# Cross attention: GpSimd in written order too, the rows' scale three steps ahead, a set's quotient ahead of its step's sums

## The chip, the cores and the metric

The kernel runs on one core of a Trainium2 chip. The metric is device time in microseconds of one execution, the median of several. Five engines work side by side, each through its own queue in order: TensorE (PE; its weight loads are listed as PEld), VectorE (DVE), ScalarE (ACT), GpSimd (POOL) and SyncE (SP), which here only issues transfers.

## What is computed

One decoder layer on x of 4 x 512 x 512 (2048 rows), in three blocks, each added to the residual:

```python
x = x + attn(layernorm(x))            # causal, window of 128, 16 heads, sink, folded output weights
x = x + xattn(layernorm(x), ctx)      # 16 query heads in 4 groups, 1024 keys, 4 batches
x = x + ffn(layernorm(x))             # ternary weights, 8-bit rows, silu gate, Hadamard turn
```

The middle block is the one that the change touches:

```python
Q, K, V = query @ Wq, key @ Wk, value @ Wv        # 16 heads of 32 over 4 groups of keys and values
scores = einsum(Q / sqrt(32), K) + slope * (k - q)  # masked keys to the least number
out = einsum(softmax(scores), V) @ Wo
```

Ahead of it and ahead of the feed-forward block each row is normalized, (x - mean) / sqrt(var + 1e-5).

## The kernel before, in words

The work of the cross attention is cut into 16 sets: set m is batch m // 4 and head hh = m % 4 of all four groups, with its 512 queries. A set has 8 tiles of 128 keys. The main loop (line 1295) takes one tile a step: step = 8 m + kt, written here as m.kt, so that step 9 is 1.1.

In a step TensorE computes scores transposed (keys on the partitions) into two score buffers (`st`, lines 1100 and 1111), ScalarE takes their exponentials `p` (line 1118, two instructions of 128 x 1024), and TensorE weighs the values with those of the step before (line 1136). GpSimd adds the exponentials of a set's tiles 1 to 7 into two sums (line 1125, two additions a step; in the last set VectorE does it). For a set further on TensorE also makes untransposed scores (line 1038, four a step), of which VectorE takes row maxima (line 1042). They are turned, copied by ScalarE and sent as two more rows of the queries (`shift`, lines 1077 to 1093), so that the exponentials can't overflow.

In step m.1 the sums of set m - 1 are added over the keys by TensorE (`divide`), copied by ScalarE, and spread by transfers; in m.2 VectorE takes reciprocals, which return by transfers; in m.4 GpSimd multiplies the set's output by them (`quotients`, line 1183). Later `output` (line 1190) multiplies by Wo and VectorE adds to the residual.

Work for later stages is laid between these steps by `plan`: turning the next batch's context, its keys and values, the queries of later sets, and two kinds of normalized rows. `rows_of(b)` (line 270) is a generator that prepares the next batch's four row tiles; each `next` runs it to its next `yield`. Its parts are: the statistics on VectorE (lines 87 and 88), `norm_of` (line 100), which has GpSimd add epsilon (`veps`, line 106) and take the power -0.5 (`rstd`, the scale of the rows, line 80); then `norm_shift` (line 110), in which ScalarE computes -mean x scale (`shift`, lines 113 and 116), for which it needs GpSimd's result; then the rows themselves (`norm_rows`, line 120), each turned by TensorE a step later. `ffn_rows` (line 331) does the same for pairs of row tiles of the feed-forward block, with three steps between `norm_of` and `norm_shift`, and then quantizes the rows; six pairs start at steps 87, 93, 102, 108, 114 and 120, which are 10.7, 11.5, 12.6, 13.4, 14.2 and 15.0.

What sets the order on an engine is `tc.manual_schedule(engines=...)`, line 1274. An engine named there issues in the order in which the program is written. For the others a planner, with its own estimates of each instruction's time, places instructions by when it believes them to be ready, and may move them ahead of what is written before them. In the kernel before only TensorE is named in the cross attention. Whatever the order, each engine's queue is worked off from the front, and an instruction that waits for another engine's result holds all behind it.

Of the kernel before, what the change touches and what calls it, by code (L numbers as in the profile page):

```python
# [50 lines left out]
def decoder_layer(  # L51
# [48 lines left out]
    def norm_of(t0, n):  # L100

        mv = row_stats(t0, n)
        veps, rstd, shift = (
            small.tile([P, QT], F32, name=name, bufs=1) for name in ("veps2", "rstd2", "shift")
        )
        nc.gpsimd.tensor_tensor(veps[:, :n], mv[:, :n, 1], least[:, 0, :n], ALU.add)
        power_neg_half(rstd[:, :n], veps[:, :n])
        return mv, rstd, shift, n

    def norm_shift(mv, rstd, shift, n):  # L110

        for i in range(n):
            nc.scalar.activation(
                shift[:, i:i + 1], mv[:, i, 0:1], AF.Copy, scale=rstd[:, i:i + 1]
            )
        nc.scalar.activation(shift[:, :n], shift[:, :n], AF.Copy, scale=-1.0)
        return rstd, shift

    def norm_rows(dst, t, i, rstd, shift):
        nc.scalar.activation(  # L120
            dst, xres[:, t, :], AF.Identity, bias=shift[:, i:i + 1], scale=rstd[:, i:i + 1]
        )
# [66 lines left out]
    def transpose4(src, dst, copy):  # L189
        ps = some_bank([P, DC, P], "tr_ps")  # L190
        for c in range(DC):
            nc.tensor.transpose(ps[:, c, :], src[:, ts(c, P)], ident)
        copy(dst, ps)
# [73 lines left out]
                    )  # L267
            nc.scalar.copy(self.va[:, 2 * quarter:2 * quarter + 2, :], v_ps)

    def rows_of(b):  # L270

        hT = bx.tile([P, DC, T], F32, name="h2T")
        hTs[b] = hT
        norm = norm_of(b * QT, QT)
        yield
        rstd, shift = norm_shift(*norm)
        ahead = None
        for i in range(QT + 1):
            if i < QT:
                h = bx.tile([P, D], F32, name="h2", bufs=2)  # L280
                norm_rows(h, b * QT + i, i, rstd, shift)
            if ahead is not None:
                transpose4(ahead, hT[:, :, ts(i - 1, P)], nc.scalar.copy)
            ahead = h
            yield
# [207 lines left out]
    with tc.tile_pool(name="aw", bufs=1) as aw, tc.tile_pool(name="akv", bufs=2) as akv, \  # L493
# [289 lines left out]
        class Unit:  # L783
# [42 lines left out]
            def weights(self):  # L826
                s, nm, es = self.s, self.nm, self.es
                self.p = a2.tile([P, HG, P], F32, name="p")
                den = small.tile([P, HG], F32, tag="den", name="den")
                for h in range(HG):  # L830
                    nc.scalar.activation(  # L831
                        self.p[:, h, :], s[:, h, :], AF.Exp, bias=nm[:, h:h + 1],
                        scale=self.rs[:, h:h + 1], accum_out=den[:, h:h + 1],
                    )
                nc.scalar.activation(es, es, AF.Exp)
                nc.vector.tensor_tensor(den, den, es, ALU.add)
                nc.vector.reciprocal(den, den)  # L837
                nc.gpsimd.tensor_tensor(  # L838
                    self.p, self.p, den.unsqueeze(2).to_broadcast([P, HG, P]), ALU.mult
                )  # L840
# [57 lines left out]
        with tc.manual_schedule(  # L898
            engines={mybir.EngineType.PE, mybir.EngineType.Activation, mybir.EngineType.DVE}
# [105 lines left out]
    with tc.tile_pool(name="b1", bufs=1) as b1, \  # L1005
# [61 lines left out]
        def merge(m):  # L1067

            full = small.tile([P, QT, G, 2], F32, tag="nm3", name="nm3", bufs=2)
            both = nms[m].rearrange("p q g h -> p (q g) h").unsqueeze(2)  # L1070
            nc.vector.tensor_reduce(
                full.rearrange("p q g h -> p (q g) h"), both.to_broadcast([P, QT * G, 2, 2]),
                AX.X, ALU.min,
            )
            nms[m] = full
# [106 lines left out]
        def quotients(m):  # L1182
            nc.gpsimd.tensor_tensor(oTs[m], oTs[m], recs[m], ALU.mult)

        def quotient(m, qt):
            rec, o = recs[m][:, ts(qt, P)], oTs[m][:, ts(qt, P)]
            nc.vector.reciprocal(rec, rec)
            nc.vector.tensor_tensor(o, o, rec, ALU.mult)
# [16 lines left out]
        SETS = B * HG  # L1205
        extra, at_end = {}, {}

        def plan(step, what, *args, to=extra):
            to.setdefault(step, []).append(lambda: what(*args))
# [11 lines left out]
        def side_queries(m, half):  # L1221
            if half == 0:
                nms[m] = small.tile([P, QT, G, 2], F32, tag="nm2", name="nm2", bufs=2)
            queries(m, half)
            if half == 1:
                send_queries(m)

        for b in range(1, B):
            at = KT * HG * (b - 1)
            rows_two = rows_of(b)  # L1230
            for what, when in (
                ("turn", (0, 4, 9, 16)), ("keys", (1, 5, 12, 20)), ("values", (8, 13, 24, 28))
            ):
                for quarter, step in enumerate(when):
                    if step < 2 and b == 1:
                        step -= 2
                    plan(at + step, side_work, b, what, quarter)
            for step in range(11, 17):
                plan(at + step, lambda rows_two=rows_two: next(rows_two, None))
        for m in range(SETS):  # L1240
            for half in range(2 if m > 1 else 0):
# [29 lines left out]

        with tc.manual_schedule(engines={mybir.EngineType.PE}):
            nms[0] = small.tile([P, QT, G, 2], F32, tag="nm2", name="nm2", bufs=2)
            first.values(0)
            first.turn(2, nc.scalar)
            first.keys(2)
            first.values(1)
            side_queries(1, 0)  # L1280
            first.turn(3)
            first.keys(3)
            first.send(1)
            for i in range(G * QT):
                row_maxima(0, i)
                if i == 2:
                    side_queries(1, 1)
                if i in (5, 8):
                    first.values(2 + i // 8)
                if i == 8:  # L1290
                    batches[1] = KeysValues(1)
                    batches[1].rows()
            merge(0)
            last = None
            for step in range(-2, KT * SETS):
                m, kt = divmod(step, KT)
                now = 0 <= step < KT * SETS
                ahead, i0 = divmod(step + 10, KT)
                maxima = [
                    lambda i=i: row_max(ahead, 4 * i0 + i) for i in range(4)  # L1300
                ] if 0 <= ahead < SETS else []
                for f in maxima[:3]:
                    f()
                sts = [scores(m, kt, 0)] if now else None
                for f in maxima[3:]:
                    f()
                if now:
                    sts.append(scores(m, kt, 1))
                for f in extra.pop(step, []):
                    f()  # L1310
                if maxima and i0 == KT - 1:
                    merge(ahead)
                ps = weights(m, kt, sts) if now else None
                if last is not None:
                    weigh(*divmod(step - 1, KT), last)
                if kt == 1 and 1 <= m < SETS:
                    divide(m - 1, before_last)
                    spread(m - 1)
                if kt == 2 and 1 <= m < SETS:
                    reciprocals(m - 1)  # L1320
                if kt == 4 and 1 <= m < SETS:
                    quotients(m - 1)
                for f in at_end.pop(step, []):
                    f()
                before_last, last = last, ps
            ternary_load("d")
            weigh(SETS - 1, KT - 1, last)
            divide(SETS - 1, last)
            scores_pool.close()
            gup = ctx.enter_context(tc.tile_pool(name="cgu", bufs=4, space=PSUM, side="right"))  # L1330
            tiles = [Tile(t) for t in range(NT)]
            tiles[0].gated_mm(0)
            tiles[0].gated_mm(1)
            for qt in range(QT):
                quotient(SETS - 1, qt)
            for n in range(2):
                tiles[0].gated_mul(n)
                tiles[0].gated_mm(n + 2)
                output(SETS - 2, (2 * n, 2 * n + 1), 2)
            for n in range(2, 4):  # L1340
                tiles[0].gated_mul(n)
            for half in range(2):
                tiles[0].first(half)
# [6 lines left out]
    with tc.tile_pool(name="c1", bufs=1) as c1, \  # L1350
# [5 lines left out]
                engines={mybir.EngineType.PE, mybir.EngineType.DVE, mybir.EngineType.Activation}  # L1356
# [109 lines left out]
```

## Time and profile before

| what | us |
|---|---|
| median of 3 runs | 1684.91 (1684.77 to 1685.11) |
| the profiled execution | 1685.37 |
| its span, first to last instruction | 1683.6 |
| PE busy | 1617.5 (96%) |
| DVE busy | 1183.3 (70%) |
| ACT busy | 925.0 (55%) |
| POOL busy | 716.5 (43%) |
| granted TensorE clock, mean | 0.990 |
| cross attention, first to last exponentials | 724 to 1382 |

The page is one profiled execution. Busy time is a union over the engine's instructions; a busy TensorE is not TensorE at its peak, since matmuls are pipelined. Lines are those of the kernel before. A row of the timeline gives start, length, engine, line, operation, output and inputs, shape, count, and in brackets the idle time of the engine just before with what ended it. A row of the waits gives engine and line that waited, what it waited for, the sum in us, how often, and the longest.

### The profile page before, as it was taken

What the parts mean: (1) busy time and instruction counts of PE and PEld (TensorE: products, weight loads), DVE (VectorE), ACT (ScalarE), POOL (GpSimd) and SP (SyncE); (2) the same over time, 40 slices, a digit from 0 to 9 for tenths busy, and PEclk for the clock granted to TensorE, in tenths of its full rate; (3) what the DMA queues carried; (4) which work ended last, traced back from release to release, by engine and by line L of the source; (5) the groups of instructions that cost most, each with busy time, mean ns of one, the idle gap of its engine ahead of it and who ended that gap; (6) DMA issues with size and microseconds to landing.
All of it is one profiled execution on the core that took longest, in us unless ns stands there. A gap on an engine that the chain in (4) does not pass through costs nothing.

```text
span 1683.6 us, 23520 instructions
## 1 busy us (share of the span) xinstructions
PE 1617.5 (96%) x8096; PEld 954.3 (57%) x8128; DVE 1183.3 (70%) x2357; ACT 925.0 (55%) x1871; POOL 716.5 (43%) x480
## 2 busy tenths in 40 slices
PE   7999999999999999799999999999989998999997
PEld 4566666655666665555555555555544435666664
DVE  4566887987778762665666565666657657999997
ACT  1554454555446562145444554445656765888886
POOL 1212232322223221268888787878769930000000
PEclk9999999999999999799999999999989999999999
DMA  8531312322223101421212121211122110000000
GB/s 260 153 110 54 100 52 71 82 84 82 69 82 88 50 1 36 109 51 39 58 27 71 39 58 26 67 44 39 33 66 58 38 57 3 13 14 13 20 13 32
DMA packets 96552, 99.61 MB, mean 59 GB/s; under 512 B 50884, under 2 KB 57672, under 8 KB 96008
## 3 DMA queue, kind: packets, MB, share of 16 engines
q1 hardware_dynamic: 88320, 83.77, 17.8%
q10 hardware_dynamic: 6960, 13.17, 2.4%
q0 software_dynamic: 1152, 1.15, 0.3%
q8 instruction: 64, 1.05, 0.3%
q14 instruction: 56, 0.46, 0.1%
HBM read 61.76 MB, written 10.86 MB: 43 GB/s over the span
## 4 chain that ended last, share of the span: by engine, by line
PE 79%; DVE 9%; ACT 5%; issue 3%; DMA 2%; POOL 1%; SPq 1%; ACTq 0%; DVEq 0%; POOLq 0%
PE y L683 12%; PE s_ps L1038 8%; PE st L1100 7%; PE o_ps L1136 6%; PE sc L809 5%; PE q_ps L295 3%; PE st L1111 3%; PE xo_ps L1195 3%; PE q_ps L790 3%; PE av L869 3%; PE f_ps L671 3%; PE d_ps L477 2%; PE y_ps L429 2%; PE u_ps L393 2%; PE g_ps L393 2%
## 5 line engine op out<-in xcount | busy, mean ns | idle before, releaser
L1125 POOL TENSOR_TENSOR sum<-sum,p 128x1024 f32<-128x1024 f32 x180 | 422.5, 2376 | 36.2 <-ACT p L1118 36.0
L1042 DVE TENSOR_REDUCE nm<-s_ps 128x1 f32<-128x512 f32 x480 | 300.0, 681 | 160.2 <-PE s_ps L1038 159.9
L1118 ACT ACTIVATE p<-st 128x1024 f32<-128x1024 f32 x256 | 249.3, 1020 | 96.0 <-PE st L1111 89.6
L683 PE MATMUL y<-wf,attnT 128*128 128x512 f32 x512 | 251.7, 602 | 0.0
L838 POOL TENSOR_TENSOR p<-p,den 128x512 f32<-128x512 f32 x64 | 67.0, 1046 | 356.5 <-DVE den L837 194.6
L1038 PE MATMUL s_ps<-ks,qs 99*128 99x512 f32 x480 | 184.2, 454 | 17.2 <-DVE nm L1042 10.4
L1038 PEld LDWEIGHTS s_ps<-ks,qs 99*128 99x128 f32 x480 | 82.2, 190 | 159.8 <-DVE nm L1042 50.8
L1100 PE MATMUL st<-qs,ks 101*128 101x512 f32 x512 | 164.8, 403 | 6.3 <-ACT p L1118 5.8
L1136 PE MATMUL o_ps<-p,va 128*32 128x512 f32 x1024 | 137.7, 608 | 0.0
L831 ACT ACTIVATE p<-s,nm,rs 128x128 f32<-128x128 f32 x256 | 123.2, 484 | 8.9 <-DVE nm L821 7.2
L683 PEld LDWEIGHTS y<-wf,attnT 128*128 128x128 f32 x512 | 88.0, 190 | 61.6 <-issue 59.1
L1125 POOL TENSOR_TENSOR sum<-p,p 128x1024 f32<-128x1024 f32 x30 | 70.5, 2372 | 108.5 <-ACT p L1118 80.2
L1100 PEld LDWEIGHTS st<-qs,ks 101*128 101x128 f32 x512 | 95.7, 191 | 35.7 <-ACT p L1118 20.2
L809 PE MATMUL sc<-kT,qT 128*128 128x256 f32 (+1 forms) x512 | 107.6, 353 | 0.0
L809 PEld LDWEIGHTS sc<-kT,qT 128*128 128x128 f32 x512 | 88.6, 190 | 25.8 <-issue 15.5
L80 POOL TENSOR_TENSOR rs<-ss,neghalf 128x4 f32<-128x4 f32 (+1 forms) x72 | 81.7, 1135 | 43.5 <-DVE ss L588 39.9
L802 ACT COPY qT<-qtr 128x512 f32<-128x512 f32 x64 | 37.5, 585 | 113.4 <-PE qtr L800 113.4
L883 ACT COPY attnT<-av 128x256 f32<-128x256 f32 x128 | 42.7, 375 | 82.0 <-PE av L875 74.7
L393 PEld LDWEIGHTS <-xqT 128*128 128x128 bf16 x512 | 50.0, 98 | 47.8 <-issue 1.4
L299 ACT ACTIVATE qH<-q_ps 128x256 fp32r<-128x256 f32 x32 | 12.3, 384 | 102.2 <-PE q_ps L295 97.2
L429 PE MATMUL y_ps<-had,mT 128*128 128x128 f32 x512 | 68.2, 281 | 0.0
L790 PE MATMUL q_ps<-wqu_sb,qcT 128*128 128x512 f32 x128 | 66.4, 600 | 0.0
(203 smaller groups left out, 3057.2 us busy)
## 6 DMA issues: line engine op xcount, KB each, us to landing
qs<-qH SPq DMA_DIRECT2D x128, 64.0 KB
cx<-in_ctx SPq DMA_DIRECT2D x30, 256.0 KB
w<-in_L_attn_out_w SPq DMA_DIRECT2D x16, 256.0 KB
w<-in_L_attn_out_w SPq DMA_DIRECT2D x4, 1024.0 KB
raw<-in_L_ffn_w_gate SPq DMA_DIRECT2D x4, 1024.0 KB
raw<-in_L_ffn_w_up SPq DMA_DIRECT2D x4, 1024.0 KB
raw<-in_L_ffn_w_down SPq DMA_DIRECT2D x4, 1024.0 KB
raw<-in_L_ffn_w_gate ACTq DMA_DIRECT2D x8, 512.0 KB
```

Of the source, the lines that this page charges most:

```text
L393: nc.tensor.matmul(acc, lhsT=xqTs[self.t][:, c, :], rhs=w[c][:, ts(n, 512)], start=(c == 0), stop=(c == DC - 1),)
L429: nc.tensor.matmul(y_ps[:, k, :], lhsT=self.mT[q][:, k, :], rhs=had, start=True, stop=True)
L683: nc.tensor.matmul(y, lhsT=attnT[:, h, :], rhs=wf[:, h, :], start=(h == 0), stop=(h == HEADS - 1))
L790: nc.tensor.matmul(q_ps, lhsT=made[self.b][0][:, ts(self.qt, P)], rhs=wqu_sb[:, ts(self.g, HG * P)], start=True, stop=True,)
L809: nc.tensor.matmul(sc[:, h, first * P:], lhsT=self.qT[:, h, :], rhs=kT[:, (qt - 1 + first) * P:(qt + 1) * P], start=True, stop=True,)
L831: nc.scalar.activation(self.p[:, h, :], s[:, h, :], AF.Exp, bias=nm[:, h:h + 1], scale=self.rs[:, h:h + 1], accum_out=den[:, h:h + 1],)
L1038: nc.tensor.matmul(s_ps, lhsT=qss[hh][0:R_TOP, g, ts(qt, P)], rhs=kss[b % 2][0:R_TOP, g, ts(hf, T)], start=True, stop=True,)
L1042: nc.vector.tensor_reduce(nms[m][:, qt, g, hf:hf + 1], s_ps, AX.X, ALU.max, negate=True)
L1100: nc.tensor.matmul(st[:, g % 2, :], lhsT=ks[0:R_TOP + 2, g, ts(kt, P)], rhs=qss[hh][0:R_TOP + 2, g, :], start=True, stop=False,)
L1118: nc.scalar.activation(p, st, AF.Exp)
L1125: by.tensor_tensor(sums[m][i], last[i] if kt == 1 else sums[m][i], ps[i], ALU.add)
L1136: nc.tensor.matmul(accs[m][at, :], lhsT=va[:, kt, at], rhs=ps[g // 2][:, g % 2, :], start=(kt == 0), stop=(kt == KT - 1),)
```

## The change

GpSimd joins TensorE in written order inside the cross attention, so that its additions, the rows' scale, the quotients and the transfers that it issues now stand as the program has them. With that, two pieces are moved in the text. The generator of a batch's rows starts at step 9 of the batch before (m.1 of its second set) instead of 11 and yields three times instead of once between the scale and the shift; the shift and all behind it are still written at steps 12 to 16. And the quotient is written ahead of the exponentials and sums of its step instead of behind them. VectorE, ScalarE and SyncE stay with the planner. No computation is added or left out.

```diff
-    def rows_of(b):
+    def rows_of(b, apart=1):
...
         norm = norm_of(b * QT, QT)
-        yield
+        for _ in range(apart):
+            yield
         rstd, shift = norm_shift(*norm)
...
-            rows_two = rows_of(b)
+            rows_two = rows_of(b, 3)
...
-            for step in range(11, 17):
+            for step in range(9, 17):
                 plan(at + step, lambda rows_two=rows_two: next(rows_two, None))
...
-        with tc.manual_schedule(engines={mybir.EngineType.PE}):
+        with tc.manual_schedule(engines={mybir.EngineType.PE, mybir.EngineType.Pool}):
...
+                if kt == 4 and 1 <= m < SETS:
+                    quotients(m - 1)
                 ps = weights(m, kt, sts) if now else None
...
-                if kt == 4 and 1 <= m < SETS:
-                    quotients(m - 1)
```

## The prediction

> **What bounds the kernel now.** I read the page's busy rows first, then the windows of the cross attention, then who waited for whom there, then the timelines of the engines around the longest of those waits.
>
> ```profile
> PE 1617.5 (96%) x8096; PEld 954.3 (57%) x8128; DVE 1183.3 (70%) x2357; ACT 925.0 (55%) x1871; POOL 716.5 (43%) x480
> L1125 POOL TENSOR_TENSOR sum<-sum,p 128x1024 f32<-128x1024 f32 x180 | 422.5, 2376 | 36.2 <-ACT p L1118 36.0
> ...
> ACT shift L113 <- POOL rstd L80: 10.2, 3, 5.4
> ```
>
> TensorE has 96% of the span and is full in every stage, so time is gained or lost only where something makes it stand. POOL's 43% is an average that misleads: in the cross attention it adds two tiles per step, 2 x 2.376 us, in seven steps of a set, and one quotient of 1.28 us, about 34.5 us in a set of 36 to 43 us. A result asked of POOL there comes late, behind the sums already queued. The last line (ScalarE's waits inside the cross attention) is the only place where that now hurts: 10.2 us in 3 waits of the rows' shift for the rows' scale. The two long ones, as the timelines of ScalarE, POOL and TensorE show them (start, length, engine, line, in brackets the idle time before):
>
> ```profile
> 1217.26 1.92 ACT L1118 ACTIVATE p<-st 128x1024 f32<-128x1024 f32 x2
> 1219.06 0.81 ACT L120 ACTIVATE h<-xres,shift,rstd 128x512 f32<-128x512 f32 x1
> 1225.30 0.48 ACT L113 ACTIVATE shift<-mv,rstd 128x1 f32<-128x1 f32 x2 [5.42 <-POOL rstd L80]
> ...
> 1237.22 0.81 ACT L120 ACTIVATE h<-xres,shift,rstd 128x512 f32<-128x512 f32 x1
> 1241.98 0.29 ACT L113 ACTIVATE shift<-mv,rstd 128x1 f32<-128x1 f32 x1 [3.94 <-POOL rstd L80]
> ```
>
> ```profile
> 1215.24 9.37 POOL L1125 TENSOR_TENSOR sum<-sum,p 128x1024 f32<-128x1024 f32 x4
> 1224.57 0.69 POOL L80 TENSOR_TENSOR rstd<-veps,neghalf 128x2 f32<-128x2 f32 x1
> ...
> 1228.83 1.39 PE L1038 MATMUL s_ps<-ks,qs 99*128 99x512 f32 x2 [4.12 <-DVE nmT L1089]
> ...
> 1243.24 0.73 PE L1100 MATMUL st<-qs,ks 101*128 101x512 f32 x2 [2.37 <-ACT p L1118]
> ```
>
> The exponentials of a step ended at 1219.17, its sums at 1224.60 (that step's two are the end of the 9.37 us run), the scale behind them at 1225.26; the shift had to wait, and with it all that ScalarE had queued, the next exponentials first. TensorE stood 4.12 and 2.37 us, and the windows around these gaps give its granted clock (columns: stretch, its length, busy time of PE, PEld, DVE, ACT and POOL with counts, granted clock, DMA share, GB/s):
>
> ```profile
> 1228.80:1233.90 5.10, 5.07 (x10) 3.14 (x11) 2.55 (x4) 5.05 (x11) 3.35 (x2) 0.50 0.11 29
> 1244.20:1247.60 3.40, 3.40 (x15) 1.14 (x18) 0.69 (x1) 3.40 (x8) 0.00 (x0) 0.50 0.00 0
> 683.20:687.80 4.60, 4.51 (x11) 3.65 (x12) 0.21 (x1) 0.48 (x1) 2.35 (x5) 0.50 0.29 68
> ```
>
> Behind every gap over 2 us (the third line follows one of 3.6 us at 679.7) it ran at half clock for 3.4 to 5.1 us, so a gap costs 1.7 to 2.55 us on top of itself.
>
> **The pattern to look for.** Both long waits have one form: in ScalarE's queue the shift stands directly behind the exponentials of step X (here set 11, tiles 5 and 7), in POOL's queue the scale stands behind the sums of the same step X. The sums need 2 x 2.36 us after the exponentials have come, and end 3.92 us behind them at best, so that order contains a stall of some 5 us. Where the scale stands at least a step ahead, nothing waits: in set 1 it follows the sums of tile 5, the shift follows the exponentials of tile 6, and the shift started at 795.38 without idle time.
>
> **What the built program says.** POOL now follows the written order, ScalarE and VectorE are still placed by the planner, TensorE's order is unchanged, and so is SyncE's. Counting instructions in the built queues, the shift stands behind the exponentials of step X and the scale behind the sums of the same X in all nine places but the last: tile 7 of sets 0, 4 and 8 (rows of batches 1 to 3), then 10.7, 11.5, 12.6, 13.4, 14.2 (set.tile; the feed-forward rows, first five pairs). For the last pair the scale follows the sums of 14.7, the shift the exponentials of 15.0. The three steps of distance exist in the source but not in ScalarE's queue, because the planner pulls the shift up to where it believes the scale to be ready.
>
> **Part by part.**
>
> *Removed:* the two stalls. From the exponentials of step 11.5 to those of 12.1 it took 1246.34 - 1217.26 = 29.08 us; the same steps a set later, with the same side work, 1286.11 - 1267.16 = 18.95. Gain 10.1 us.
>
> *Added:* nine waits. How late the next exponentials start: lag of the sums behind the step's exponentials (L), plus offset and power on POOL (0.20 + 0.08 + 1.03 = 1.31 us for four columns as at 793.57; 0.20 + 0.08 + 0.70 = 0.98 for two), plus what ScalarE does between the shift and the next exponential in the built order (w), minus the time from the exponentials' end to the next ones' start today (n), minus TensorE's slack: at step 1.0 the first exponential ends at 761.30 and TensorE's next scores, which need its buffer, start at 761.91, so 0.6. w is four shifts 0.85, negation 0.2, two rows of 0.82 + 0.72 and a copy of 0.3 = 2.9 us for a batch; 1.8 for the first pair; 2.65, 2.2, 0.65 and 0.65 for the next. L and n from the timelines:
> - 0.7: 6.46 + 1.31 + 2.9 - 3.72 - 0.6 = 6.35
> - 4.7 and 8.7: 3.92 + 1.31 + 2.9 - 3.59 - 0.6 = 3.94 each
> - 10.7: 3.93 + 0.98 + 1.8 - 3.95 - 0.6 = 2.2
> - 11.5: 5.43 + 0.98 + 2.65 - 3.72 - 0.6 = 4.7 (n from the undisturbed 12.5)
> - 12.6: 4.48 + 0.98 + 2.2 - 3.49 - 0.6 = 3.6
> - 13.4: 6.26 + 0.98 + 0.65 - 1.67 - 0.6 = 5.6
> - 14.2: 4.70 + 0.98 + 0.65 - 1.66 - 0.6 = 4.1
> - 15.0: 0 to 2.6, since POOL will have caught up during the wait before; 1.5 taken.
>
> Sum 35.9 us. The same arithmetic gives the two old stalls 2.9 + 2.5, with half clock (2.55 + 1.7) 9.7, against 10.1 measured, so I trust it to a tenth.
>
> *The clock.* Seven gaps are over 3 us; from the rows above I take 2.4 us each, and 1.7 for the one of 2.2: 18.5 us. The Trainium skill (TensorE: Matmul & The Clock Gate, "Why this matters for your kernels") says that only idle gaps over some 3 us drop the clock, and under "What's actually happening" that one busy window of about 3.4 us restores it: 1.7 us for each of seven, 11.9 us, a total 6.6 us lower. The rows disagree twice: a gap of 2.37 us was followed by half clock, and 5.1 us of work ran slowly behind another. The rows decide.
>
> *At nothing:* the quotient stands in the built queue where the planner had put it, behind the sums of tile 3 (in set 14 one addition earlier): no cost. POOL's three transfers of key rows for batches 2 and 3 are issued together, up to 4.7 us later, behind the sums of 3.7 and 7.7; their first readers, the row maxima, start over 20 steps on. POOL's small operations only change place (in set 1, one pair for another; three more in all, 1.5 us). The shift and two rows of batch 1 leave ScalarE at 634 to 637 us, where the chain that ended last runs over TensorE: between 0 and -0.7, taken as 0; if that cover were gone, the 0.7 would be a gain.
>
> *What queues behind each new wait:* on ScalarE the copy of v, the exponentials, the row-maxima's transposed copy; then TensorE, whose score buffers are two, then VectorE's maxima. POOL loses nothing by it: it catches up.
>
> Sum: 35.9 + 18.5 - 10.1 = +44.3 us. The profiled execution, span 1683.6, took 1685.37 us, 0.5 above the median of 1684.91; on the median the forecast is 1729 us.
>
> **The rivals.**
> - *Nine waits, clock as the rows show* (0.72): 1729, own range 1714 to 1744.
> - *Nine waits, the clock stays up* (0.10): 35.9 - 10.1 = +25.8, 1711. For it: gaps of about 1 us at 1307 leave the clock alone. Against it: three of three longer ones did not.
> - *VectorE joins* (0.10): in its queue the peaks of the feed-forward rows wait for rows that now come late, and the row maxima stand behind them. Six pairs, each four maxima of 0.62 us to catch up: 6 x 2.5 = 15 more, 1744. Against it: TensorE mostly stands then anyway.
> - *Faster* (0.06): TensorE has more work in hand than the 0.6 us I read. With slack s instead, the nine late times sum to the 10.1 us saved at s = 3.8 us, nearly a whole step; beyond it the change wins: at 4.5 us, 5.3 - 10.1, 1680. Against it: a ScalarE wait of 3.94 us did leave TensorE idle for 2.37.
> - *The change does nothing measurable* (0.02): the old waits merely exchanged for equal ones, within 0.2% (3.4 us, about what a measurement of this kernel can tell from no change). Nine against two speaks against it.
>
> **How the numbers follow.** Slower 0.92, same 0.02, faster 0.06. Low end: slack of 1.0 instead of 0.6 takes 3.5 us from nine places and no clock loss 18.5 more: 1707. High end: 2.55 for each big gap, 2.6 at the last place, and VectorE's 15: about 1747. Together these leave some 2 in 10 outside 1707 to 1746.
>
> **What would show it.** ScalarE's waits should name the shift waiting for the scale about nine times, some 50 us in all, instead of 10.2; TensorE should show gaps of 2 to 6.5 us behind steps 0.7, 4.7, 8.7, 10.7, 11.5, 12.6, 13.4, 14.2, each followed by half clock, and a mean clock near 0.98 instead of 0.99. Sets 11 and 12 should have lost the old pattern behind 11.7. If the shifts start without idle time the forecast is wrong at its root; if they wait but TensorE doesn't, the slack was misread.

## The result, and the profile after

The changed kernel takes 1729.45 us (median of 4 runs, 1728.23 to 1730.35) against 1685.01 us for the kernel before (4 runs, 1684.77 to 1688.95). The ratio is 1.0259, 95% interval 1.0245 to 1.0273: 44.4 us slower. The profiled execution has a span of 1726.4 us at a mean granted clock of 0.980; before it was 1683.6 us at 0.990.

The same three lines as shown of before: the page's busy rows, its group of GpSimd's additions, and ScalarE's waits inside the cross attention (who waited for whom: total, times, longest). Behind line 276 the changed file is one line longer, so that L1118 of before is L1119 here.

```profile
PE 1635.4 (95%) x8128; PEld 961.6 (56%) x8128; DVE 1184.6 (69%) x2357; ACT 926.1 (54%) x1871; POOL 716.8 (42%) x480
L1126 POOL TENSOR_TENSOR sum<-sum,p 128x1024 f32<-128x1024 f32 x180 | 422.5, 2374 | 51.7 <-ACT p L1119 51.5
...
ACT shift L113 <- POOL rstd L80: 49.4, 9, 7.7
```

No engine has more work; TensorE's busy time grew by 17.9 us, 17.8 of them inside the cross attention, where it has the same 3476 matmuls but ran more of them at half clock. What is new is the last line: nine waits of the shift for the scale, 49.4 us, where there were three of 10.2. GpSimd itself now waits longer for ScalarE (51.7 us of idle time in that group instead of 36.2): it stands because the exponentials it is to add come late, and catches up.

The first of the nine places, behind the exponentials of step 0.7, in the timelines of ScalarE, GpSimd and TensorE (start, length, engine, line, idle time before in brackets):

```profile
751.66 1.94 ACT L1119 ACTIVATE p<-st 128x1024 f32<-128x1024 f32 x2 [1.77 <-PE st L1112]
761.34 0.85 ACT L113 ACTIVATE shift<-mv,rstd 128x1 f32<-128x1 f32 x4 [7.74 <-POOL rstd L80]
...
762.46 1.52 ACT L120 ACTIVATE h<-xres,shift,rstd 128x512 f32<-128x512 f32 x2
763.89 0.35 ACT L268 COPY va<-v_ps 128x256 f32<-128x256 f32 x1
764.14 1.93 ACT L1119 ACTIVATE p<-st 128x1024 f32<-128x1024 f32 x2
```

```profile
750.70 9.34 POOL L1126 TENSOR_TENSOR sum<-sum,p 128x1024 f32<-128x1024 f32 x4
...
760.28 1.03 POOL L80 TENSOR_TENSOR rstd<-veps,neghalf 128x4 f32<-128x4 f32 x1
```

```profile
758.13 0.73 PE L1039 MATMUL s_ps<-ks,qs 99*128 99x512 f32 x2
764.29 0.79 PE L1039 MATMUL s_ps<-ks,qs 99*128 99x512 f32 x1 [5.43 <-ACT va L268]
```

ScalarE's exponentials ended at 753.60. It then had nothing else to do than the shift, which stands next in its queue, and the shift's scale stood in GpSimd's queue behind the sums of that very step, which ended at 760.04. Behind the shift come two rows, the copy of v and the next exponentials; TensorE resumed when the copy of v was there, 5.4 us late. This is the order that the prediction described, at the same instructions.

The granted clock behind three of the gaps (windows: stretch, its length, busy time and number of PE, PEld, DVE, ACT and POOL, granted clock, DMA share, GB/s):

```profile
763.20:766.60 3.40, 2.18 (x4) 1.46 (x5) 0.69 (x1) 3.35 (x6) 0.00 (x0) 0.50 0.00 0
766.60:770.00 3.40, 3.40 (x15) 2.36 (x13) 1.24 (x2) 0.59 (x1) 0.00 (x0) 0.50 0.07 16
...
1121.70:1125.00 3.30, 3.30 (x12) 2.69 (x12) 0.73 (x2) 1.38 (x3) 0.00 (x0) 0.50 0.00 0
1336.70:1346.90 10.20, 6.33 (x23) 2.86 (x23) 4.15 (x8) 6.84 (x11) 5.29 (x3) 0.50 0.00 1
```

All nine places against the prediction. "Excess" is by how much the time between the end of one step's exponentials and the end of the next ones' grew against before, summed over the two to five steps at the place. The last column is the length of the stretch of half clock there, from the trace's own records of the clock; all columns but the first are in us.

| behind step | lateness forecast | TensorE's gap | excess forecast (with clock) | excess measured | half clock |
|---|---|---|---|---|---|
| 0.7 | 6.35 | 5.43 | 8.75 | 8.36 | 6.83 |
| 4.7 | 3.94 | 3.01 | 6.34 | 5.41 | 3.41 |
| 8.7 | 3.94 | 3.14 | 6.34 | 5.11 | 3.41 |
| 10.7 | 2.2 | 0.90 + 1.12 | 3.9 | 5.25 | 6.83 |
| 11.5 | 4.7 | 4.08 + 1.66 | 7.1 - 10.1 = -3.0 | -1.97 | 6.83 |
| 12.6 | 3.6 | 3.34 | 6.0 | 6.01 | 6.83 |
| 13.4 | 5.6 | 7.85 | 8.0 | 9.17 | 10.24 |
| 14.2 | 4.1 | 2.62 | 6.5 | 4.57 | 3.41 |
| 15.0 | 1.5 | 1.40 | 1.5 | 2.49 | 3.41 |
| sum | 35.9 | 34.5 | 44.3 | 44.4 | |

From the end of step 0.0's exponentials to those of 15.7 the kernel took 45.3 us longer; 44.4 of them lie in this table.

### The profile page after: what moved, and what is told of

Its sections match the earlier page's. It is cut to its first block, busy times and chain, and to the rows that moved or that the text cites. A ratio compares the mean times of both kernels' runs of the same rounds, so it can differ in the third digit from the quotient of the medians.

```text
span 1726.4 us, 23536 instructions
## 1 busy us (share of the span) xinstructions
PE 1635.4 (95%) x8128; PEld 961.6 (56%) x8128; DVE 1184.6 (69%) x2357; ACT 926.1 (54%) x1871; POOL 716.8 (42%) x480
## 4 chain that ended last, share of the span: by engine, by line
PE 76%; DVE 9%; ACT 6%; POOL 3%; issue 3%; DMA 2%; SPq 0%; ACTq 0%; DVEq 0%; POOLq 0%
PE y L684 11%; PE s_ps L1039 7%; PE st L1101 6%; PE sc L810 5%; PE o_ps L1137 5%; PE q_ps L296 3%; PE st L1112 3%; PE xo_ps L1196 3%; PE q_ps L791 3%; PE av L870 3%; PE f_ps L672 3%; POOL sum L1126 3%; PE d_ps L478 2%; ACT p L1119 2%; PE y_ps L430 2%
## 5 line engine op out<-in xcount | busy, mean ns | idle before, releaser
L1126 POOL TENSOR_TENSOR sum<-sum,p 128x1024 f32<-128x1024 f32 x180 | 422.5, 2374 | 51.7 <-ACT p L1119 51.5
L1119 ACT ACTIVATE p<-st 128x1024 f32<-128x1024 f32 x256 | 249.4, 1020 | 101.0 <-PE st L1112 97.6
L1101 PE MATMUL st<-qs,ks 101*128 101x512 f32 x512 | 170.9, 416 | 12.8 <-ACT p L1119 12.1
L80 POOL TENSOR_TENSOR rs<-ss,neghalf 128x4 f32<-128x4 f32 (+1 forms) x72 | 81.8, 1136 | 42.8 <-DVE ss L589 39.4
L1112 PE MATMUL st<-qL,kL 32*128 32x512 f32 x512 | 66.3, 506 | 0.0
```

What stands on the lines that cost most here:

```text
L1101: nc.tensor.matmul(st[:, g % 2, :], lhsT=ks[0:R_TOP + 2, g, ts(kt, P)], rhs=qss[hh][0:R_TOP + 2, g, :], start=True, stop=False,)
L1112: nc.tensor.matmul(sts[g // 2][:, g % 2, :], lhsT=kL[at, ts(kt, P)], rhs=qLs[m][at, :], start=False, stop=True,)
L1119: nc.scalar.activation(p, st, AF.Exp)
L1126: by.tensor_tensor(sums[m][i], last[i] if kt == 1 else sums[m][i], ps[i], ALU.add)
```

## The experiments

### Which part of the change costs it

The change has three parts: GpSimd in written order, the rows' plan with the scale three steps ahead, and the quotient's place. Three kernels take them apart, and a fourth makes the supposed cause larger.

**The flag alone** (the kernel before, with GpSimd in written order):

```diff
-        with tc.manual_schedule(engines={mybir.EngineType.PE}):
+        with tc.manual_schedule(engines={mybir.EngineType.PE, mybir.EngineType.Pool}):
```

> Only GpSimd's written order, on the kernel before; rows' scale and quotient stay where they were written. In the built queues each of the nine shifts again stands directly behind the exponentials of the step whose sums stand ahead of its scale (batch rows now at tiles 1.2, 5.2, 9.2; the pairs as in the changed kernel). Theory (the stalls come from written order on GpSimd with the planner still placing ScalarE): nine waits, ScalarE's shift waits 45 to 50 us in all, time 1722 to 1734. Rival (the moved generator and its three steps cost the time): about 1685.

Measured: 1728.04 us (1727.22 to 1729.13), ratio 1.0252 (1.0237 to 1.0267). ScalarE's waits in it:

```profile
ACT shift L113 <- POOL rstd L80: 46.9, 9, 7.5
```

The batches' three waits stand three steps later there (behind 1.2, 5.2 and 9.2, where the plan of before has these rows: 6.2, 6.8 and 5.7 us of excess), the six of the feed-forward rows stayed where they are in the changed kernel. The flag alone costs 42.5 us (1685.59 for the kernel before in the same series), the whole change 44.4, and the intervals of their ratios overlap.

**The moves alone** (the changed kernel, with GpSimd left to the planner):

```diff
-        with tc.manual_schedule(engines={mybir.EngineType.PE, mybir.EngineType.Pool}):
+        with tc.manual_schedule(engines={mybir.EngineType.PE}):
```

> Only the moves (rows' scale from step 9 with three yields, quotient ahead of its step's sums), GpSimd left to the planner. Theory: the planner places scale and shift as in the kernel before, two long waits of about 5.4 and 3.9 us stay, time 1685, within 3 us. Rival (the moves cost the time): 1700 or more. A third reading (the moves alone remove the old stalls): about 1675.

Measured: 1685.2 us (1682.48 to 1687.19), ratio 0.9996 (0.9988 to 1.0005). The shift's waits are those of the kernel before, with TensorE's gaps of 4.14 and 2.36 us:

```profile
ACT shift L113 <- POOL rstd L80: 10.2, 3, 5.4
```

Where the planner places GpSimd's instructions, the places in the source do nothing measurable.

**The quotient behind its step's sums again** (the changed kernel otherwise):

```diff
-                if kt == 4 and 1 <= m < SETS:
-                    quotients(m - 1)
                 ps = weights(m, kt, sts) if now else None
...
                 if kt == 2 and 1 <= m < SETS:
                     reciprocals(m - 1)
+                if kt == 4 and 1 <= m < SETS:
+                    quotients(m - 1)
```

> The changed kernel with the quotient written behind its step's sums again. GpSimd then does the quotient 4.7 us later in each of 14 sets. Theory: nine waits as in the changed kernel; in the sets whose output follows two steps behind the quotient (three of four heads) TensorE may wait about 1 us for it, so 1729 to 1740. Rival (the quotient's place is part of the loss): below 1727.

Measured: 1727.99 us (1723.82 to 1728.52), ratio 1.0246 (1.0229 to 1.0263), with nine waits of 49.6 us. That is 1 us under the 1729 to 1740 that I expected: only steps 3.6 and 7.6 take longer, by 0.8 us each, and the interval overlaps that of the changed kernel. The quotient's place is worth nothing that can be measured.

**The scale later still**: three more powers on GpSimd ahead of each scale inside the cross attention, into a tile that the shift overwrites. Nothing of the computation is left out.

```diff
+        for _ in range(3 if inside else 0):
+            power_neg_half(shift[:, :n], veps[:, :n])
         power_neg_half(rstd[:, :n], veps[:, :n])
```

> The changed kernel with three more powers of the same size on GpSimd ahead of each scale (results unused): each scale comes later by 3 x 1.1 us for the three batches and 3 x 0.75 for the six pairs, in all 3 x 3.3 + 6 x 2.25 = 23 us. Theory (TensorE has no more than 0.6 us in hand, every further us of wait is paid in full): plus 21 to 30 us with the clock, so 1750 to 1760. Rival (TensorE has work in hand, the loss is the clock or VectorE): plus less than 10 us.

Measured: 1752.65 us (1751.62 to 1753.85), ratio 1.0400 (1.0383 to 1.0417). ScalarE's waits:

```profile
ACT shift L115 <- POOL rstd L80: 71.8, 9, 10.9
```

22.4 us more of waiting cost 23.2 us more time. Inside the cross attention TensorE was idle 19.5 us longer than in the changed kernel (68.9 against 49.4) and busy 2.8 us longer, with 75.1 us at half clock against 51.2. At the three batches its gap grew by 3.2 us each, about as much as the scale came later; at 15.0 by 0.4 us only. So at most of these places TensorE has no reserve left that a later scale would first use up.

### Taking the wait away: the scale on VectorE

If the wait for GpSimd is the cause, a scale that doesn't come from GpSimd removes it. The kernels of this kind leave out the power and compute a reciprocal in its place, so their rows are scaled by another number.

```diff
-        nc.gpsimd.tensor_tensor(veps[:, :n], mv[:, :n, 1], least[:, 0, :n], ALU.add)
-        power_neg_half(rstd[:, :n], veps[:, :n])
+        nc.vector.tensor_tensor(veps[:, :n], mv[:, :n, 1], least[:, 0, :n], ALU.add)
+        nc.vector.reciprocal(rstd[:, :n], veps[:, :n])
```

On the changed kernel:

> The changed kernel with the rows' scale taken off GpSimd: VectorE adds epsilon and takes a reciprocal where GpSimd took the power -0.5 (so the rows are scaled by another number; all else is computed as before). GpSimd's written order stays. Theory (a scale that is queued behind the sums is the whole cause): all nine waits go, and the two old ones with them, 1685 - 10 = 1675, at most 3 us less for a freer start of the cross attention. Rival (written order on GpSimd costs by itself, through sums, quotients or transfers): 1685 or more.

and on the kernel before:

> The kernel before with the rows' scale on VectorE in the same way (a reciprocal in place of the power). Theory: only the two old waits go, 1685 - 10 = 1675, the same as the changed kernel with that edit within 3 us. If written order on GpSimd is worth something by itself, the two differ.

Measured: 1683.44 us (1681.73 to 1685.91), ratio 0.9994 (0.9987 to 1.0001), and 1684.15 us (1680.23 to 1686.93), ratio 0.9989 (0.9980 to 0.9998). No shift waits for a scale any more, and the whole loss of 44 us is gone. The two times lie within 1 us of each other, so GpSimd's written order by itself, with its sums, quotients and transfers, costs nothing that can be measured. But both should also have been rid of the two old stalls in sets 11 and 12, some 10 us, and most of that was missing. VectorE's timeline (first lines), GpSimd's and TensorE's show where it went in the first of the two:

```profile
1220.18 0.15 DVE L107 RECIPROCAL rstd<-veps 128x2 f32<-128x2 f32 x1
...
1220.38 5.99 DVE L106 TENSOR_TENSOR veps<-mv,least 128x2 f32<-128x2 f32 x1
1226.29 0.73 DVE L1090 SCALAR_TENSOR_TENSOR nmT<-nm_ps,parts,nmT 8x512 fp32r<-8x512 f32 x1
```

```profile
1212.35 14.00 POOL L1126 TENSOR_TENSOR sum<-sum,p 128x1024 f32<-128x1024 f32 x6
```

```profile
1227.08 1.40 PE L1039 MATMUL s_ps<-ks,qs 99*128 99x512 f32 x2 [5.24 <-DVE nmT L1090]
```

The addition of epsilon to two columns took 5.99 us instead of the 0.15 us that it takes where GpSimd is idle. It ended at 1226.37, and GpSimd's run of six additions at 1226.35. On the kernel before it is the same: 5.97 us, ending 0.02 us behind GpSimd's run. Behind the held addition, in VectorE's queue, stood the maxima's turned copy, and TensorE waited 5.24 us for it. So the old stall was gone, and a new one stood in nearly the same place.

My first reading was that the addition was held for its two inputs in SBUF, and that one with a constant would pass:

```diff
+        nc.vector.tensor_scalar(veps[:, :n], mv[:, :n, 1], LN_EPS, None, ALU.add)
+        nc.vector.reciprocal(rstd[:, :n], veps[:, :n])
```

> As the changed kernel with the scale on VectorE, but epsilon is added as a constant, so that VectorE's instruction reads one tile from SBUF instead of two (the rows are again scaled by a reciprocal, another number than the reference's). In the run with two inputs one such addition of 128x2 took 5.99 us and ended 0.02 us after a run of GpSimd additions; TensorE stood 5.24 us behind it. Theory (an instruction of VectorE with two SBUF inputs can't pass while GpSimd's additions follow each other): no addition of epsilon over 0.3 us, no gap over 2 us in the cross attention, 1674 to 1678. Rival (the gap has another cause, as the row maxima's shift waiting in VectorE's queue): the gap of 5 us stays and the time is 1683.

Measured: 1683.43 us (1681.9 to 1685.9), ratio 0.9988 (0.9980 to 0.9996). A miss: VectorE's timeline and GpSimd's have

```profile
1225.33 6.00 DVE L106 TENSOR_SCALAR veps<-mv 128x2 f32<-128x2 f32 x1
```

```profile
1217.31 13.99 POOL L1126 TENSOR_TENSOR sum<-sum,p 128x1024 f32<-128x1024 f32 x6
```

held again, to 1231.33, where GpSimd's run ended at 1231.30. The reading of two inputs was too narrow. The Trainium skill (SBUF — State Buffer, "Who interferes with whom") says that VectorE and GpSimd share one pair of SBUF ports as an exclusive lock, that VectorE needs it for an instruction with two SBUF inputs and also for a `tensor_scalar` that runs in a two-port mode, and that the one which comes second is blocked outright. Both forms were held here; whether this `tensor_scalar` ran in such a mode no trace shows. What should then pass is an instruction with one SBUF input and no such mode, and the reciprocals beside GpSimd's additions took 0.15 to 0.18 us. So the next kernel leaves the addition of epsilon out:

```diff
-        nc.gpsimd.tensor_tensor(veps[:, :n], mv[:, :n, 1], least[:, 0, :n], ALU.add)
-        power_neg_half(rstd[:, :n], veps[:, :n])
+        nc.vector.reciprocal(rstd[:, :n], mv[:, :n, 1])
```

> The changed kernel with the rows' scale on VectorE as its reciprocal of the variance alone: GpSimd's addition of epsilon and its power are both left out, and nothing on VectorE takes the addition's place. So the scale is 1/variance instead of the inverse root of variance plus epsilon, and the output differs from the reference for that. Theory (what held VectorE for 6 us in the three kernels with the scale on VectorE was the addition of epsilon alone, not the scale's being there; reciprocals beside GpSimd's additions took 0.15 to 0.18 us): no VectorE operation of two columns over 1 us, no TensorE gap over 2 us in the cross attention, some 6 to 10 us less than 1683: 1673 to 1678. Rival (any small VectorE operation between scale and shift is held until GpSimd's additions have ended): the reciprocal itself takes some 6 us at set 11 and the time stays at 1683.

Measured: 1675.23 us (1672.53 to 1675.83), ratio 0.9936 (0.9923 to 0.9949). All nine scales, from the trace's view of line 106 (count, shortest, median and longest in ns), and the one at set 11, inside a GpSimd run from 1214.07 to 1228.11:

```profile
L106 DVE RECIPROCAL rstd<-mv x9: 146/157/179, 791.6 to 1400.6; 128x2 f32<-128x2 f32 x7, 128x4 f32<-128x4 f32 x2
...
1221.90 0.15 DVE L106 RECIPROCAL rstd<-mv 128x2 f32<-128x2 f32 x1
```

TensorE has no gap above 1.2 us left in the cross attention, its clock is full there throughout, and the cross attention is 9.4 us shorter than before (9.2 of it in steps 11.6 to 12.1). That is about the size of the two old stalls, which the prediction put at 10.1 us. With and without the addition of epsilon the changed kernel differs by 8.2 us, 6.8 of it inside the cross attention.

### Taking the wait away: ScalarE in written order too

The other half of the pattern is that the planner pulls the shift up. With ScalarE in written order as well, the distance in the source holds in its queue:

```diff
-        with tc.manual_schedule(engines={mybir.EngineType.PE, mybir.EngineType.Pool}):
+        with tc.manual_schedule(engines={mybir.EngineType.PE, mybir.EngineType.Pool, mybir.EngineType.Activation}):
```

> The changed kernel with ScalarE in written order too. In the built queue the shifts then stand three steps and more behind their scales (behind the exponentials of 1.3, 5.3, 9.3, 11.2, 12.0, 13.1, 13.7, 14.5, 15.3). Theory: no wait of a shift for a scale is left; 1672 to 1680 if ScalarE's written order costs nothing else. Rival: its written order brings waits of its own (copies and quantizing steps ahead of exponentials), then 1685 to 1710, with other names in ScalarE's waits.

Measured: 1682.47 us (1679.22 to 1686.01), ratio 0.9980 (0.9972 to 0.9987): faster than both kernels, by less than the 1672 to 1680 that I expected. No shift waits for a scale. Of about 9 us gained at steps 11.6 to 12.0, most is given back in the profiled execution (1684.62 us): 1.8 us each at steps 1.4, 5.4, 5.5 and 9.4, of which 0.9 us each return at 1.6, 5.6 and 9.6, and 7 us in the last ten steps. Where it goes shows in TensorE's busy time over the whole cross attention, in the kernel with the reciprocal alone (first line) and in this one (ten matmuls lack a record in it); the columns are those of the windows above:

```profile
723.23:1371.55 648.32, 631.90 (x3476) 336.39 (x3476) 402.53 (x687) 355.59 (x492) 515.12 (x231) 1.00 0.18 47
722.26:1378.61 656.35, 640.08 (x3466) 338.51 (x3467) 402.33 (x679) 361.76 (x499) 524.22 (x249) 0.99 0.18 47
```

TensorE's idle time is as low as with the reciprocal alone, 656.35 - 640.08 = 16.3 us against 16.4; its busy time is 8.2 us longer, and by the trace's records of the clock 19.5 us of the stretch ran at half clock, against none. 16.1 us of these lie in the last ten steps, where TensorE has gaps of 1.66, 0.89 and 1.32 us. So the stalls are gone and the clock takes the gain. ScalarE has a new wait, 7.2 us in 6 times for VectorE's inverse of the rows' maxima, but only 3.2 us of it in the last ten steps. What makes each of the small gaps there was not tried.

So the order was written only where the rows are. In both kernels the main loop's body becomes a function, called in three stretches; the middle one has TensorE, GpSimd and ScalarE in written order, the others TensorE alone. First from step 10.6 to 14.7:

```diff
+            for step in range(-2, 86):
+                before_last, last = one_step(step, before_last, last)
+        with tc.manual_schedule(engines={mybir.EngineType.PE, mybir.EngineType.Pool, mybir.EngineType.Activation}):
+            for step in range(86, 120):
+                before_last, last = one_step(step, before_last, last)
+        with tc.manual_schedule(engines={mybir.EngineType.PE}):
+            for step in range(120, KT * SETS):
+                before_last, last = one_step(step, before_last, last)
```

> The kernel before, with GpSimd and ScalarE in written order for steps 86 to 119 alone (10.6 to 14.7, where the five first pairs of feed-forward rows lie) and only TensorE in written order ahead of and behind that. In the built queues each shift there stands at least three steps behind its scale. Theory: the two old waits go and no other comes, steps 0 to 85 and 120 to 127 as in the kernel before: 1685 less 8 to 10 us, 1675 to 1678. Rival (ScalarE's written order costs in these steps what it saves): 1682 to 1686.

Measured: 1683.84 us (1681.18 to 1687.8), ratio 0.9992 (0.9983 to 1.0000): a miss. Steps 11.6 to 12.0 gained 8.4 us, and steps 14.6 and 14.7 lost 8.6. The timelines of GpSimd, ScalarE and TensorE there:

```profile
1337.56 4.64 POOL L1125 TENSOR_TENSOR sum<-sum,p 128x1024 f32<-128x1024 f32 x2
1342.16 0.70 POOL L80 TENSOR_TENSOR rstd<-veps,neghalf 128x2 f32<-128x2 f32 x1
...
1342.89 0.29 ACT L113 ACTIVATE shift<-mv,rstd 128x1 f32<-128x1 f32 x1 [5.16 <-POOL rstd L80]
...
1344.75 2.12 PE L1100 MATMUL st<-qs,ks 101*128 101x512 f32 x4 [6.99 <-ACT p L1118]
```

The last pair of rows lies in the stretch left to the planner, and the planner had moved them forward, its scale to the end of the sums of step 14.5 and its shift to that of the exponentials: the same pattern as before, made anew. In the second kernel the middle stretch therefore reaches to step 15.3 (`range(86, 124)`), so that all six pairs lie inside:

> The kernel before, with TensorE, GpSimd and ScalarE all in written order from step 86 to step 123 (sets 10.6 to 15.3, so that all six pairs of feed-forward rows lie inside), and TensorE alone elsewhere as before. In the built queues the scale now stands two or three quarters of a step to a full step apart from its shift: at 10.7 and 11.2, 11.5 and 12.0, 12.6 and 13.1, 13.4 and 13.7, 14.2 and 14.5, 14.7 and 15.3. Theory (the loss lies only in a shift that stands right behind the exponentials of the step whose sums the scale stands behind): no wait of a shift for a scale over 1 us, steps 94 to 96 about 8 us shorter, steps 118 and 119 without the 8.6 us that the shorter stretch cost: 1676 to 1680. Rival (ScalarE in written order costs elsewhere what it saves, as it did in the last sets with all of the cross attention written): 1683 or more.

Measured: 1681.2 us (1675.56 to 1684.1, 9 runs), ratio 0.9973 (0.9964 to 0.9983). No shift waits for a scale, and steps 11.6 to 12.0 gain 8.4 us. Of this 6.1 us are given back: 2.6 us at steps 14.6 and 14.7, 1.0 at 12.6 and 2.5 in the last steps, so the time lies above the 1676 to 1680 that I expected, and below the rival's 1683. The largest piece, in the timelines of ScalarE and TensorE:

```profile
1332.43 0.48 ACT L113 ACTIVATE shift<-mv,rstd 128x1 f32<-128x1 f32 x2
...
1333.18 1.52 ACT L120 ACTIVATE h<-xres,shift,rstd 128x512 f32<-128x512 f32 x2
...
1335.83 1.90 ACT L1118 ACTIVATE p<-st 128x1024 f32<-128x1024 f32 x2
```

```profile
1336.88 0.73 PE L1100 MATMUL st<-qs,ks 101*128 101x512 f32 x2 [1.68 <-ACT p L1118]
```

The shift starts without idle time, but it, both rows and the maxima's copies stand ahead of the exponentials, and TensorE stood 1.68 us. Here too the idle time over the cross attention is down to 16.5 us, and TensorE was busy 4.7 us longer than with the reciprocal alone: 10.2 us ran at half clock, behind this gap and one of 0.90 us. The intervals of this kernel and of the one with ScalarE written throughout overlap, so which of them is faster is open; of the kernels here that leave nothing of the computation out, these two gain most.

## Why the prediction was right

**The pattern and its nine places: right.** Nine waits of the shift for the scale were forecast, some 50 us; there are nine, 49.4 us, each at the step named. That they are the cause is shown from both sides: the flag alone makes them and the loss, more lateness costs as much as it adds, and two unrelated ways of taking them away (scale on VectorE, ScalarE in written order) take the whole loss away.

**The lateness of each place: right in the sum, off by up to 2 us in single places.** 35.9 us were forecast, the gaps of the table sum to 34.5. Where the batches' rows come (0.7, 4.7, 8.7) the gap is 0.8 to 0.9 us smaller, because TensorE could resume with one matmul when the copy of v was there, ahead of the exponentials that I had counted to; at 4.7 and 8.7 it then stood another 0.42 us for these, which the table leaves out. At 14.2 the gap is 1.5 us smaller than the lateness: the exponentials do start 4.6 us late (6.27 us behind the ones before, 1.66 in the kernel before), but TensorE had 2.0 us of work in hand there, not the 0.6 us read at step 1.0 and taken for all nine places. At 13.4 it is 2.2 us larger, for TensorE's next matmuls waited not for the exponentials but for something behind them on ScalarE:

```profile
1336.27 0.48 ACT L113 ACTIVATE shift<-mv,rstd 128x1 f32<-128x1 f32 x2 [7.18 <-POOL rstd L80]
...
1336.89 1.92 ACT L1119 ACTIVATE p<-st 128x1024 f32<-128x1024 f32 x2
1338.70 0.81 ACT L120 ACTIVATE h<-xres,shift,rstd 128x512 f32<-128x512 f32 x1
1339.40 1.11 ACT L327 ACTIVATE xqT<-xq_ps,magic 128x1024 bf16<-128x1024 bf16 x1
...
1340.57 0.79 PE L1039 MATMUL s_ps<-ks,qs 99*128 99x512 f32 x1 [7.85 <-ACT xqT L327]
```

The exponentials ended at 1338.81, the copy of the turned rows at 1340.51. The term w of that place counts only what stands ahead of the exponentials and so leaves out the row and the copy behind them, 1.7 of the 2.2 us.

**The clock: undersized by 3.3 us, and the rows were still the better guide.** 18.5 us were taken from three stretches of before. A better measure is TensorE's busy time over the cross attention: before, after and in the kernel with the reciprocal alone (whose line stands above) it is that of the same 3476 matmuls, and in the last of these the clock is full throughout. Before and after:

```profile
724.23:1381.96 657.73, 635.82 (x3476) 338.03 (x3476) 402.39 (x679) 355.65 (x492) 521.34 (x246) 0.99 0.18 47
721.26:1424.27 703.01, 653.66 (x3476) 346.04 (x3476) 403.37 (x679) 358.73 (x499) 523.75 (x249) 0.96 0.17 44
```

Against the 648.32 us with the reciprocal alone, before is 9.4 us longer. The changed kernel is idle for 49.4 us against 16.4, which is 32.9 us more, and busy for 653.66 - 631.90 = 21.8 us more. So the sum that came out is 32.9 + 21.8 - 9.4 = 45.3 us, where 35.9 + 18.5 - 10.1 = 44.3 was forecast. The waits were taken 3.0 us too large and the clock 3.3 us too small, and at the single places of the table misses of up to 1.9 us add up to 4.5 us in each direction. The mechanism was right; that the total met the forecast within 1 us is luck. (Each of these is one profiled execution.)

Excess less gap at the eight places without 11.5, where the old stalls are mixed in, leaves 46.4 - 28.8 = 17.6 us, 2.2 each, against 16.1 forecast for these eight; this remainder also holds whatever else changed in those steps. The rule that only gaps over some 3 us count would have left three places out (10.7, 14.2, 15.0), and all three were followed by half clock: behind a gap of 2.62 us, of 1.40 us, and behind two of 0.90 and 1.12 us within 3 us. The prediction had taken no clock loss at 15.0, and at 10.7 one for a single gap of 2.2 us.

**The removed stalls: right.** -10.1 us was the forecast; the kernel without any wait of the shift or held addition is 9.2 us faster at these steps. In the changed kernel the gain is hidden, since a new wait stands at the same place: steps 11.6 to 12.2 come out 2.0 us shorter, where -3.0 was forecast.

**The quotient and the transfers: right at nothing**, the quotient by its own experiment. The transfers weren't tried by themselves; no wait for them shows at the nine places.

**The start of the cross attention: left open.** Its first exponential starts 3.0 us earlier than before (721.26 against 724.23), where 0 to -0.7 was forecast. The kernel with the moves alone has -2.9 there too, but in the others it lies between -6.6 and +2.3, without order in what they change. There is one profile of each kernel, so how far it scatters between executions of the same kernel isn't shown, and nothing is read from it. In this one profile it takes 3.0 us off the 45.3 by which the cross attention grew, and the span is 42.8 us longer.

**The rivals.** The clock stays up: refuted by the windows. VectorE joins: TensorE's waits for VectorE's maxima are 8.8 us in the cross attention, 9.4 before, so VectorE didn't fall behind. It only carried one wait further: behind 11.5 its peaks waited for the late rows, a residual addition stood behind them, and TensorE waited 4.1 us for that, in place of the 4.1 us that it stood there before. Faster: it needed 3.8 us of reserve in TensorE's work at each place; the largest that was seen is the 2.0 us at 14.2, and the kernel with later scales had little left to use up.

One thing the prediction asserted without a test was that the planner pulls the shift up to where it believes the scale ready. That the shift stands there is in the queues and in the trace; the planner's belief was not looked at. In the first kernel with a stretch in written order it did the same with another pair of rows.

## What to carry to other kernels

Putting one more engine into written order does not hold a distance between two instructions if the second is on an engine that is still placed by a planner: ask for each handover where both ends stand in the built queues, and look for a consumer that stands right behind work on which its producer's queue is busy. An engine that is 43% busy over the whole run may be full in the one stage where a small result is asked of it, and the small result then costs as much as the queue ahead of it plus a stretch of half clock. Moving the small operation to another engine helps only if that engine can run it beside the busy one: look at its duration there, not only at its place. And count the small gaps that a new order brings: the two kernels with ScalarE in written order left TensorE no more idle than the best one, and half of the gain or more still went into half clock.

## What the runs showed of the hardware that was not expected

VectorE's additions of 128 x 2 and 128 x 4 elements, in SBUF with two inputs or with one input and a constant, were held while GpSimd added: 5.99, 5.97 and 6.00 us in three kernels instead of 0.15, and about 0.8 and 1.65 us at other places, each ending 0.01 to 0.03 us behind an addition of GpSimd. The three long ones began inside the fourth of six additions that followed each other without a pause and were released only at the end of the sixth, though two additions ended meanwhile: the hold lasted as long as additions stood back to back. In the trace each of these additions begins 0.03 to 0.05 us before the one ahead of it has ended, which may be why; that was not tried. Reciprocals of the same sizes beside such additions took 0.15 to 0.18 us.

In the changed kernel half clock also followed gaps as short as 1.40 us, and a pair of 0.90 and 1.12 us, and its stretches were 3.41, 6.83 or 10.24 us long. The length of a gap alone does not settle it: with ScalarE in written order TensorE had three gaps of 1.02 us in the same place of three batches (steps 1.4, 5.4 and 9.4), and half clock followed the second alone. The stretches behind the second and the third:

```profile
956.36:959.77 3.41, 3.41 (x17) 3.32 (x17) 0.49 (x2) 0.00 (x0) 3.33 (x2) 0.50 0.00 0
1128.80:1132.40 3.60, 3.60 (x25) 3.05 (x25) 1.29 (x3) 0.98 (x2) 3.58 (x2) 1.00 0.15 36
```
